# Two tiles of rows, each loaded in two halves of 64 rows through two queues

## The chip, the core and the metric

The kernel runs on one core of a Trainium2 chip. The core has a TensorE for matrix products (PE in the profile, with its weight loads as PEld), a VectorE (DVE), a ScalarE (ACT), a GpSimd (POOL) and a SyncE (SP); transfers between the chip's memory and the core's are started by instructions on the queues of SyncE, ScalarE or GpSimd, and are carried out by 16 DMA engines. The metric is the device time of one execution in microseconds, as the median of several runs.

## The reference

Two layers are computed on 2 x 512 rows of 512 numbers, in single precision, and only the final rows are returned. Cut to what matters:

```
x = L0_attn_hidden_states                       # (2, 512, 512)
x = layernorm(x + L0_attn(x))                   # linear attention with a fixed memory M, z
x = layernorm(x + L0_ffn(x))                    # gated, weights of three values, integers inside
x = layernorm(x + L1_attn(x))                   # softmax attention, one head of 128
x = layernorm(x + L1_ffn(x))                    # gated, 1376 wide

# L0_attn: of 32 query heads only every fourth is used (8 heads of 128)
q   = hidden @ Wq.T + bq ; sig_q = elu(q) + 1
num = sig_q @ M[h] ;  den = sig_q . z[h] + 1e-6
out = repeat(num / den, 4) @ Wo.T
```

What is changed lies ahead of the first product, the queries q of layer 0.

## The kernel before

The rows are held as eight tiles of 128 rows by 512 columns, `x_b_t` with batch b of 0 and 1 and tile t of 0 to 3 (256 KB each). TensorE needs them turned, so each 128 x 128 block is transposed by a matmul against an identity.

The queries of the first head and first batch are computed plainly, tile by tile, in `first_queries`: `first_rows(t)` transposes the four blocks of tile t (L454), then ScalarE copies one half of the result to `xt_raw` (L456) and VectorE the other (L457), and the same result is split into an upper and a lower part for the later heads (`xh_a` by ScalarE, L326; `xl_a` by VectorE, L327). Then four matmuls with the weights `wq[0]` (L473) add up the queries of that tile. All other heads are computed from split parts: `query_weights` splits a head's weights in three (ScalarE at L319, VectorE at L320 and L321, into `host_y` for head 1), and `passes` multiplies (L502), over the 512 rows of a batch at once. Behind them come the folding of M with Wo (L543), the reading of the memory (L557), the three other sublayers, and the stores of the eight output tiles (L1358, L1367).

At the very start TensorE has no data. It runs eight matmuls of ones (L113, the tile `rise`), each recorded as two passes, while the first rows are on their way.

Loads are issued in a written order. SyncE's queue issues, in this order: `x_0_0`, `wq0`, `x_0_2`, `x_0_3`, `wq1`, the small `bq` and `z`, `wq2`, the four tiles of batch 1, `wq3` to `wq7` (L385), `m`, and then the large weights. ScalarE's queue issues one load, `x_0_1`, as its first instruction, ahead of the loading of its function table. GpSimd issues none of these.

The framework gives each load issued by SyncE or ScalarE the next of eight completion counters in turn. An issue waits until the transfer that used its counter last has landed. So the first eight transfers go out without such a wait, and each later one stands behind the landing of the eighth transfer before it: `wq2`, the ninth, waits for `x_0_0`; `x_1_0` for `x_0_1`; `x_1_1` for `wq0`; `x_1_2` for `x_0_2`; `x_1_3` for `x_0_3`; `wq3` for `wq1`. The framework also puts the waits that order the work between the engines: the first transpose waits for `x_0_0` and the identity, the first transpose of the second tile for `x_0_1`, and so on.

The order of the other instructions on each engine is fixed when the kernel is built, partly by a scheduler with its own estimates and partly by hand (`issue_after`). Each engine works through its list in order.

Of the kernel before, what the change touches and what calls it, by code (L numbers as in the profile page):

```python
# [19 lines left out]
P = 128  # L20
# [19 lines left out]
def kernel(  # L40
# [19 lines left out]
    nc = tc.nc  # L60
# [27 lines left out]
    def load_x(b, tiles=range(NT)):  # L88
        for t in tiles:
            x = xp.tile([P, HID], F32, tag="x", name=f"x_{b}_{t}")  # L90
            eng = nc.scalar if b == 0 and t == 1 else nc.sync
            eng.dma_start(x, x_in[b, ts(t, P), :])
            xs[b].append(x)

    load_x(0, range(2))
    bq = const.tile([D, NH], F32, tag="bq", name="bq")
    z = const.tile([D, NH], F32, tag="z", name="z")
# [281 lines left out]
    with tc.tile_pool(name="a0w", bufs=1) as a0w, tc.tile_pool(name="a0", bufs=2) as a0:  # L379
        wq = []  # L380
        for h in range(NH):
            if h % 2 == 0:
                two = query_tile(f"wq{h}").rearrange("p a (k d) -> p a k d", k=NK)
            w = two[:, h % 2]
            nc.sync.dma_start(w, wq_in[h])  # L385
            wq.append(w)
            if h == 0:
                load_x(0, range(2, NT))
            elif h == 1:
                nc.sync.dma_start(bq, bq_in)  # L390
                nc.sync.dma_start(z, z_in)
            elif h == 2:
                load_x(1)
# [819 lines left out]
    t = NT - 1  # L1213
# [248 lines left out]
```

## Time and profile before

| | us |
|---|---|
| median of 3 runs (lowest, highest) | 459.4 (459.14, 459.92) |
| the profiled execution | 459.37 |
| its span, first to last instruction | 457.6 |
| TensorE busy in it | 449.9 (98%) |
| first matmul of ones; first transpose of rows | 1.05; 4.63 |
| `wq1` issued; landed | 2.59; 7.59 |
| ScalarE's first split of weights (L319) starts | 7.61 |
| first matmul from split parts (L502) starts | 11.33 |
| loads `x` on SyncE: issue to landing, median of 7 | 4.5 |
| load `x_0_1` on ScalarE: issue to landing | 3.3 |

The granted TensorE clock is 0.998 of full speed over the span. Times in the profile count from the start of the span. In a list of the chain or of the timeline the first number is the start, the second the length, both in us; in a list of waits the numbers are the total, how many times, and the longest; in a list of one line's instructions they are the shortest, median and longest duration in ns, and then the first and the last start in us. An instruction that issues a transfer stands under the queue's name (SPq, ACTq); the transfer itself is counted from the issue to its landing.

### The profile page before, as it was taken

To read this page: it belongs to the slowest core of one execution; us is meant where nothing else is said; L and a number is where in the kernel's file an instruction comes from. 1 tells how busy PE (TensorE), PEld (TensorE's weight loads), DVE (VectorE), ACT (ScalarE), POOL (GpSimd) and SP (SyncE) were. 2 spreads that over 40 slices of the span, in tenths; PEclk is the share of its full clock that TensorE was granted. 3 is DMA by queue.
4 is the path that set the end of the run, shared out by engine and by line. 5 is a ranking of instruction groups with operands and counts; after the bars stand their busy time and mean duration, and the time that the engine had idled before them with its cause. 6 is when DMAs were issued, how large, how long until landed. Compare 5 with 4: busy or idle time off the path is not lost.

```text
span 457.6 us, 5879 instructions
## 1 busy us (share of the span) xinstructions
PE 449.9 (98%) x1929; PEld 338.0 (74%) x1929; DVE 339.5 (74%) x665; ACT 270.2 (59%) x514; POOL 110.5 (24%) x149
## 2 busy tenths in 40 slices
PE   8999999999999999999999999999999999999995
PEld 8887754344588888888766578888888888888884
DVE  4966757667867888847978899795656778998632
ACT  4778995556567975567748544564755658442101
POOL 0300206565550069101362332000000000050101
PEclk9999999999999999999999999999999999999999
DMA  8999980000038101131585500000000000001001
GB/s 293 392 267 313 178 319 1 0 3 0 2 51 238 55 3 48 47 93 38 199 323 92 94 0 2 0 0 1 0 1 0 1 1 0 1 23 46 34 37 47
DMA packets 28693, 37.14 MB, mean 81 GB/s; under 512 B 16304, under 2 KB 17200, under 8 KB 28656
## 3 DMA queue, kind: packets, MB, share of 16 engines
q1 hardware_dynamic: 23216, 30.13, 19.2%
q0 software_dynamic: 1984, 5.77, 6.8%
q10 hardware_dynamic: 3456, 0.75, 0.8%
q8 instruction: 22, 0.36, 0.3%
q14 instruction: 15, 0.12, 0.1%
HBM read 32.45 MB, written 2.10 MB: 75 GB/s over the span
## 4 chain that ended last, share of the span: by engine, by line
PE 92%; DVE 3%; issue 2%; DMA 1%; ACT 1%; SPq 0%; POOL 0%; POOLq 0%; DVEq 0%
PE pm L1252 17%; PE po L557 10%; PE pq L502 9%; PE pg_f L735 9%; PE pu_f L735 9%; PE pc L1252 8%; PE pdm L1340 8%; PE pd_f L794 4%; PE pdc L1340 4%; PE pqk L1063 3%; PE pv L1080 2%; PE pot L1129 2%; PE po L1146 2%; PE psc L1019 2%; PE pmw L543 2%
## 5 line engine op out<-in xcount | busy, mean ns | idle before, releaser
L557 PE MATMUL po<-mw,q 128*128 128x512 f32 x128 | 57.1, 599 | 0.7 <-ACT den L561 0.4
L557 PEld LDWEIGHTS po<-mw,q 128*128 128x128 f32 x128 | 22.9, 189 | 33.4 <-issue 18.6
L146 POOL TENSOR_TENSOR rstd_f<-mv_f,ln_eps 128x1 f32<-128x1 f32 x15 | 4.4, 295 | 170.8 <-DVE mv_f L1355 130.2
L1252 PE MATMUL pm<-r,ugu 128*128 128x512 f32 x152 | 37.7, 389 | 0.0
L1252 PE MATMUL pm<-r,it_early 128*128 128x512 f32 x144 | 36.6, 392 | 0.0
L1252 PEld LDWEIGHTS pm<-r,ugu 128*128 128x128 f32 x152 | 28.5, 188 | 5.9
L170 ACT ACTIVATE ta_f<-y_f,below_half 128x512 int8<-128x512 f32 (+1 forms) x22 | 15.8, 720 | 27.2 <-DVE y_f L158 26.9
L1252 PEld LDWEIGHTS pm<-r,it_early 128*128 128x128 f32 x144 | 27.0, 188 | 6.0 <-issue 0.5
L579 DVE SCALAR_TENSOR_TENSOR x<-po,den,x 128x511 f32<-128x511 f32 x40 | 29.8, 745 | 2.1
L1262 DVE SCALAR_TENSOR_TENSOR ev_q<-pm,ev_q 128x512 f32<-128x512 f32 x27 | 18.5, 686 | 14.2 <-PE pm L1252 12.0
L574 POOL TENSOR_TENSOR y<-y,y 128x511 f32<-128x511 f32 x16 | 21.1, 1320 | 25.5 <-PE po L557 20.6
L761 DVE SCALAR_TENSOR_TENSOR it_f<-tb_f,ta_f 128x512 fp32r<-128x512 int16 (+1 forms) x22 | 15.2, 690 | 13.8 <-ACT tb_f L171 13.8
L735 PE MATMUL pg_f<-xh,tu 128*128 128x512 f32 x88 | 24.4, 399 | 0.0
L1261 ACT ACTIVATE ev_q<-pc 128x512 f32<-128x512 f32 x27 | 16.0, 594 | 14.1 <-PE pc L1252 14.0
L735 PE MATMUL pg_f<-xl,tu 128*128 128x512 f32 x88 | 23.6, 389 | 0.0
L735 PE MATMUL pu_f<-xh,tu 128*128 128x512 f32 x88 | 23.5, 389 | 0.0
L735 PE MATMUL pu_f<-xl,tu 128*128 128x512 f32 x88 | 23.5, 389 | 0.0
L1142 ACT ACTIVATE x<-x,off_f,rstd_f 128x512 f32<-128x512 f32 x7 | 5.7, 816 | 27.7 <-POOL off_f L1141 27.7
L561 ACT ACTIVATE den<-po,den_eps 128x1 f32<-128x1 f32 x64 | 13.9, 277 | 12.8 <-PE po L557 12.7
L349 POOL TENSOR_SCALAR td<-wd,inv_down 128x512 fp32r<-128x512 f32 x11 | 20.1, 1847 | 1.6 <-DVE inv_down L206 1.6
L794 PE MATMUL pd_f<-td,it_f 128*128 128x512 f32 x88 | 20.3, 389 | 0.0
L1252 PE MATMUL pc<-r,ugu 128*128 128x512 f32 x72 | 19.3, 390 | 0.0
(368 smaller groups left out, 1142.7 us busy)
## 6 DMA issues: line engine op xcount, KB each, us to landing
gu<-in_gu SPq DMA_DIRECT2D x20, 512.0 KB, 6.9
wd<-in_wd SPq DMA_DIRECT2D x20, 256.0 KB, 4.2
wo<-in_wo SPq DMA_DIRECT2D x8, 512.0 KB, 8.7
wo<-in_wo POOLq DMA_DIRECT2D x8, 512.0 KB, 9.8
wq<-in_wq SPq DMA_DIRECT2D x8, 256.0 KB, 4.6
x<-in_x SPq DMA_DIRECT2D x7, 256.0 KB, 4.5
out<-x SPq DMA_DIRECT2D x7, 256.0 KB, 2.0
x<-in_bo POOLq DMA_DIRECT2D x4, 256.0 KB, 5.9
```

The source lines that it names most:

```text
L170: nc.scalar.activation(a[:n], y, AF.Relu, bias=below_half[:n])
L349: eng.tensor_scalar(out, w, factor, None, ALU.mult)
L502: done = nc.tensor.matmul(p, w, x, start=(start and i == 0), stop=(i == len(todo) - 1), skip_group_check=not start,)
L557: nc.tensor.matmul(po, qs[b][h0 + j][:, ts(t, P)], mw[:, h0 + j, :], start=True, stop=True,)
L574: nc.gpsimd.tensor_add(ys[0][:, :LAST], ys[0][:, :LAST], y[:, :LAST])
L579: steps.append(nc.vector.scalar_tensor_tensor(x[:, :LAST], four[j][:, :LAST], d, x[:, :LAST], ALU.mult, ALU.add))
L735: nc.tensor.matmul(pp[a], t[:, a, i % NK, :], x2[b][i], start=(i == 0), stop=(i == 2 * NK - 1),)
L794: nc.tensor.matmul(pd, inter[b][c][:, ts(t, P)], td[c].bitcast(F32R), start=(c == 0), stop=(c == last),)
L1252: nc.tensor.matmul(p, w, x, start=(left[id(p)] == begun[id(p)]), stop=(left[id(p)] == 1))
L1261: nc.scalar.activation(ev, pc, AF.Copy, scale=CROSS)
L1262: nc.vector.scalar_tensor_tensor(ev, pm, MAIN, ev, ALU.mult, ALU.add)
L1340: nc.tensor.matmul(p[:, :w], got[j // 4][1][kind][:, j % 4], down_parts[j][kind][:, cols], start=(j == 0 and kind == kinds[0]), stop=(j == ...
```

## The change

In `load_x`, the tiles `x_0_0` and `x_0_1` are each loaded by two transfers of 64 rows (128 KB): rows 0 to 63 by SyncE's queue and rows 64 to 127 by ScalarE's. SyncE's list therefore starts with the first halves of both tiles and goes on with `wq0`; ScalarE's list starts with the two second halves. There are two transfers more in all, one on each queue. The other loads, the arithmetic and the number of the filler matmuls are as they were.

```diff
     def load_x(b, tiles=range(NT)):
         for t in tiles:
             x = xp.tile([P, HID], F32, tag="x", name=f"x_{b}_{t}")
-            eng = nc.scalar if b == 0 and t == 1 else nc.sync
-            eng.dma_start(x, x_in[b, ts(t, P), :])
+            if b == 0 and t < 2:
+
+                for eng, half in ((nc.sync, 0), (nc.scalar, 1)):
+                    at = t * P + half * P // 2
+                    eng.dma_start(x[ts(half, P // 2)], x_in[b, at : at + P // 2, :])
+            else:
+                nc.sync.dma_start(x, x_in[b, ts(t, P), :])
             xs[b].append(x)
 
     load_x(0, range(2))
```

Five lines are added, so line numbers of the changed kernel behind `load_x` are five higher.

## The prediction

> **What bounds the kernel now.** I read the first page of the profile, then the chain that ended last in order of time, then the waits, and last the first 14 us row by row, because every edit lies there. The page says which engine sets the end:
>
> ```profile
> span 457.6 us, 5879 instructions
> ...
> PE 449.9 (98%) x1929; PEld 338.0 (74%) x1929; DVE 339.5 (74%) x665; ACT 270.2 (59%) x514; POOL 110.5 (24%) x149
> ...
> PE 92%; DVE 3%; issue 2%; DMA 1%; ACT 1%; SPq 0%; POOL 0%; POOLq 0%; DVEq 0%
> ```
>
> TensorE is busy 98% of the span and is 92% of the chain. DMA is 1% of the chain, and the chain in order of time shows where that 1% lies:
>
> ```profile
> 2.12 0.43 SPq L92
> 2.55 0.04 issue
> 2.59 5.00 DMA wq<-in_wq
> 7.59 0.02 issue
> 7.61 0.63 ACT host_y L319
> ...
> 10.70 0.71 PE pq L473 x4
> 11.41 2.04 PE pq L502 x8
> ```
>
> The transfer on the chain is the weights of head 1 (call it wq1, the second load of line 385): issued by SyncE at 2.59 us and landed at 7.59. It isn't one of the two tiles that are edited. It is released to ScalarE's first step of the exact weights (L319). ScalarE works in order, so behind it stand the copies of row tiles 2 and 3 (L456), then VectorE's halves (L457), then TensorE's last four matmuls of the first head (L473, 10.70). From 11.41 on the chain is TensorE's own, without a transfer. So a microsecond by which wq1 lands later is a microsecond at the end, and the two tiles of rows count only if they reach this place. The waits of the first 14 us give the slack:
>
> ```profile
> DVE xt_raw L457 <- ACT xt_raw L456: 5.1, 2, 4.8
> ACT xt_raw L456 <- PE pt_a L454: 3.0, 1, 3.0
> ...
> ACT host_y L319 <- DMA wq<-in_wq: 0.2, 1, 0.2
> ```
>
> ScalarE stood idle for wq1 only 0.19 us (the timeline has the 0.2 as 0.19): that is all an earlier wq1 can give, since before it ScalarE is busy from 5.47 with copies that TensorE's first transposes released. What holds those transposes?
>
> ```profile
> L454 PEldq EVENT_SEMAPHORE  x1: 51/51/51, 3.9 to 3.9; - x1
> ...
> L473 PEldq EVENT_SEMAPHORE  x1: 51/51/51, 4.8 to 4.8; - x1
> ...
> 1.05 3.79 PE L113 MATMUL rise<-ones 128*128 128x128 f32 x16 [1.05 <-DVE below_half L108]
> 4.63 1.24 PE L454 MATMUL pt_a<-ident,x 128*128 128x128 f32 x8
> ```
>
> The first two lines are waits that TensorE's queue passes: at 3.9 for x_0_0, at 4.8 for the first weights. The next two are TensorE: the filler matmuls (L113) keep it busy until 4.84 by their modelled ends, and the transposes follow without a gap. x_0_0 had been there since 3.9 (issue 0.74 plus 3.2, the shortest latency of the x loads), x_0_1 since about 4.05 (0.74 plus 3.3). Both tiles are 0.5 us and more ahead of the engine that reads them.
>
> **The change part by part.** My sum is made against the profiled execution, 459.37 us: the span of 457.6 and 1.77 around it, which no edit touches. The median of the runs shown, 459.4, is 0.03 from it.
>
> *1. The tiles arrive in halves on two queues.* The bytes don't change: 256 KB each, with rows of 2 KB as before. The nearest row of the trace for such a split is the end of the kernel, where the last output tile leaves as 160 KB by SyncE and 96 KB by ScalarE, while the seven others leave whole:
>
> ```profile
> L1358 SPq DMA_DIRECT2D out<-x x7: 332/333/360, 407.8 to 448.1; - x7
> ...
> DMA to landing us min/median/max: 2.0/2.0/2.0
> ...
> DMA to landing us min/median/max: 1.8/1.9/2.0
> ```
>
> Whole tiles land in 2.0 us, the split one's parts in 1.8 and 2.0: the split gained between 0 and 0.2 us. The Trainium skill ("DMA: Bandwidth & Descriptors", "Rules for kernel authors") speaks against this change outright: two transfers to disjoint partition halves share the same DMA engines from one queue or from two, so one transfer of 128 partitions is to be used. By the row I'd book x_0_0 up to 0.2 us earlier (more is possible, since x_0_1's bytes no longer compete with it); by the rule nothing. The sum is the same by both: what is gained here lies under the filler matmuls, until 4.63 or so. If that cover were gone, it would be worth those 0.2 us. x_0_1 is now issued second on each queue, at 1.2 instead of 0.74, so at most 0.46 us later: 4.05 becomes 4.5 at the latest, and its transposes start at about 5.2. Cost 0, with 0.7 us to spare.
>
> *2. SyncE issues one load more ahead of wq0, x_0_2, x_0_3 and wq1.* One issue is 0.43 us plus a gap of 0.04, so these four go out 0.47 us later (wq1 at 3.06 instead of 2.59). ScalarE's second issue (0.41 by its own row) moves its table load from 1.19 to about 1.65, to end near 2.95; its next work comes at 5.47, so that is hidden. Does wq1 land 0.47 later? SyncE's issues before show what sets landings, since each later one stands behind one of these loads:
>
> ```profile
> SPq L92 <- DMA x<-in_x: 1.2, 2, 0.7
> ...
> SPq L385 <- DMA wq<-in_wq: 0.3, 1, 0.3
> ```
>
> By the rows of the timeline these waits end at 6.14 (x_0_2 landed), 6.94 (x_0_3) and 7.61 (wq1). The loads were issued 0.47 us apart and landed at 4.8, 6.1, 6.9 and 7.6, so 0.7 to 1.3 apart, and the time from issue to landing grew from 3.6 to 5.0. The DMA engines, not the issue, set the pace; their share in half-microsecond stretches is 1.02 to 1.21 from 2.5 to 4.5, with a dip to 0.70 at 4.5 to 5.0. The bytes ahead of wq1 are the same five tiles. So the later issue is hidden under the transfers in front of it. The bounds: all 0.47 is paid if the landing follows the issue; 0.19 is gained if wq1 comes so early that ScalarE doesn't wait. I take the value nearest to the pacing by engines, with a charge for two more transfers to be completed: the tiny loads bq and z landed 0.17 and 0.2 us after the one in front, which bounds what one more transfer with 128 rows of its own costs; the halves add no rows, so I charge a quarter of that each, 0.1 us together, an estimate. The others: wq0 is read at 5.89 (landed 4.8, at worst 5.25), x_0_2 at 6.79 (6.1, at worst 6.6), x_0_3 at 8.12 (6.9, at worst 7.4). All hidden.
>
> *3. Which issue waits for which landing.* The eight completion counters go round, so an issue waits for the eighth transfer before it. Two more transfers at the front mean that bq waits for the first half of x_0_0, z for the second, the third wq for one half of x_0_1 and x_1_0 for the other. bq had no wait and went out at 3.06; now it follows wq1 at 3.54 or when the half has landed, 3.9 at the latest by the row of before. Queued behind it on SyncE are z, wq2 and the four x_1 tiles, so wq2 goes from 4.01 to 4.5 or 4.8 and x_1_1 from 4.96 to 5.5 or 5.8. From x_1_2 on, each issue waits for the same transfer as before, the first until x_0_2's landing at 6.14, so the delay is swallowed there. wq2 is read at 11.18 (landed by about 8.6: 4.01 plus the median of 4.6), bq at 11.70 (7.76), x_1 from 13.06: over 1.3 us to spare in each. The fourth wq, at 12.84, is the closest: issued at 7.61, landed at about 12.2, and its issue hangs on wq1's landing in both kernels. Cost 0. After 11.41 the whole list of TensorE's waits has 0.4 and 0.3 us, for ScalarE and VectorE, and none for a transfer.
>
> *4. TensorE's extra waits.* Three more semaphore waits in front of the first transposes (two half tiles where there was one, twice). One takes 51 ns by the row above. They can run while the filler runs; if the one between the two tiles is paid, ScalarE's 0.19 idle before L319 takes it. Cost 0, at most 0.1.
>
> The order of all other instructions on each engine is the same in both builds. Sum: 0 + 0.1 + 0 + 0 = +0.1 us, so 459.5.
>
> **The rivals.** *wq1 follows its issue* (+0.47): for it, wq1 is the one load on the chain, with no slack, and the dip at 4.5 us says the DMA engines aren't full all the time; against it, the growing latency. It gives 459.8 to 459.9, which is within 0.2%. *wq1 gains*: if halves spread over two queues fill the slow start (78 GB/s at 1.5 to 2.0, 229 at 2.0 to 2.5), wq1 lands early and ScalarE's 0.19 is saved: 459.2. *Slower:* a load into 64 partitions moves at half the rate. The trace of before has no such load. 512 KB at the 380 GB/s of the full stretches take 1.38 us; at half rate 1.38 more, ahead of wq1 on the same engines, so wq1 lands near 9.0 and the end is 460.8 (+0.3%). It decides from 0.92 us on, that is, if the halves run below 0.6 of the rate. Against it: both halves are under way together and cover all partitions, and by the same page of the skill ("Why a DMA increments its semaphore by 16 and not by 1") 64 rows still go to all 16 engines; no run here shows it. *Faster by more than 0.2%:* no step of mine reaches 0.92 us; the named gains end at 0.19. What is left is that one profiled execution misleads me on the filler's cover or on later stages.
>
> **How the numbers follow.** 0.2% of 459.4, about what a measurement of this kernel can tell from no change, is 0.92 us. Chances: my sum 0.50, wq1 with its issue 0.10, the small gain 0.08 (all three within 0.2%: 0.68), half rate 0.20 (slower), something unseen that is faster 0.12. The time is that of the likeliest, 459.5. The range for 8 in 10: up to 460.8 for the half-rate case, down to 458.8, which is the 0.19 gained and the spread of the runs shown (459.14 to 459.92) below it.
>
> **What would show it.** In the profile after: TensorE's first transposes still at about 4.6, directly behind the filler; SyncE's issue of wq1 at 3.06 and ScalarE's L324 (L319 before) starting at 7.6 to 7.8; x_1_2's issue still near 6.1; the first L507 (L502) matmul near 11.4. If L324 starts near 8.1, landing follows issue; near 9, the halves are slow. Wrong altogether is the prediction if the start of the L507 matmuls moves by over 0.9 us, or if a stage behind 12 us changes length while its order is the same.

## The result, and the profile after

The changed kernel takes 460.5 us (median of 12 runs, 460.06 to 461.77); the kernel before took 459.52 beside it (12 runs, 459.08 to 459.92). The ratio is 1.0025, with a 95% interval of 1.0016 to 1.0034: 0.25% slower, some 1.1 us. The forecast was 459.5 and no change that can be measured. The time lies inside the stated range, but the kernel got slower, and by the prediction's own mark (the start of the L507 matmuls moving by over 0.9 us) its account of the first 12 us was wrong.

The first page of the profile after, the span and the engines' busy time:

```profile
span 459.1 us, 5882 instructions
...
PE 450.2 (98%) x1929; PEld 338.1 (74%) x1929; DVE 339.5 (74%) x665; ACT 270.2 (59%) x514; POOL 106.6 (23%) x149
```

All engines do the same work; the span is 1.5 us longer. Where it came from is seen by the starts of the stages in the two traces (us from the start of the span):

| | before | after | later by |
|---|---|---|---|
| first matmul from split parts (L502, now L507) | 11.33 | 12.45 | 1.12 |
| first matmul of the reading (L557, L562) | 62.8 | 63.9 | 1.1 |
| first matmul of the gated layer (L735, L740) | 121.7 | 122.8 | 1.1 |
| first matmul of the last layer (L1252, L1257) | 271.5 | 272.6 | 1.1 |
| last store issued (ScalarE, L1367, L1372) | 454.59 | 455.68 | 1.09 |
| end of the span | 457.6 | 459.1 | 1.5 |

Of the 1.5 us, 1.1 arise before 12.5 us and are carried on unchanged to the last store. The other 0.4 appear behind it, where nothing is computed. There SyncE ends the program with eight waits, as many as there are completion counters. What differs is how many of them are still to be passed when the last store has landed (2.0 us after its issue); the kernel before has two, the changed one all eight:

```profile
L1458 SPq EVENT_SEMAPHORE  x2: 28/28/28, 456.6 to 456.7; - x2
L1463 SPq EVENT_SEMAPHORE  x8: 27/28/28, 457.7 to 458.1; - x8
```

They start 0.06 us apart, so six more are 0.37 us. In the traces the stores take the counters in turn, like the loads, so each load that is added moves the last store's counter on by one. The number of waits left behind the last landing fits this: 2 in the five traces without an added transfer, 1 in the two with one more, 8 in the six with two more, 7 in the one with three (e5).

The other 1.1 us have to be explained from the start. The chain of the profile after, in order of time (start, length, what):

```profile
0.73 0.60 SPq L95
...
1.40 0.57 SPq L95
...
2.01 0.58 SPq L390
...
3.58 5.12 DMA wq<-in_wq
...
8.73 0.63 ACT host_y L324
...
11.82 0.71 PE pq L478 x4
12.53 2.03 PE pq L507 x8
```

It has the same shape as before, but SyncE's first three issues took 0.57 to 0.60 us where they had taken 0.38 to 0.43, and there is one more of them: wq1 went out at 3.58 instead of 2.59, and landed at 8.71 instead of 7.59. The instructions of the new line, with their durations in ns, show the halves' price on each queue:

```profile
L95 SPq DMA_DIRECT2D x<-in_x x2: 571/587/603, 0.7 to 1.4; - x2
L95 ACTq DMA_DIRECT2D x<-in_x x2: 626/736/847, 0.7 to 1.4; - x2
...
DMA to landing us min/median/max: 2.7/3.4/5.0
```

ScalarE's second took 0.85 us, and one half of the second tile needed 5.0 us, to 6.4. TensorE now waits for it, as its timeline (with the idle time before an instruction, and what ended it, in brackets) and ScalarE's show:

```profile
4.63 0.99 PE L459 MATMUL pt_a<-ident,x 128*128 128x128 f32 x4
6.46 0.66 PE L459 MATMUL pt_a<-ident,x 128*128 128x128 f32 x4 [0.85 <-DMA x<-in_x]
...
7.43 1.19 ACT L331 ACTIVATE xh_a<-pt_a 128x512 fp32r<-128x512 f32 x2
8.73 0.63 ACT L324 ACTIVATE host_y<-wq 128x512 fp32r<-128x512 f32 x1
```

ScalarE finishes with the second tile at 8.62 (it had been 7.42) and wq1 is there at 8.71. Two things are late by over a microsecond at the same place, and either would give nearly the whole 1.1 us. The experiments had to take them apart, and to find out why an issue of half the bytes takes longer.

### The profile page after: what moved, and what is told of

The parts are those of the page before. It is cut to its first block, busy times and chain, and to the rows that moved or that the text cites. A ratio compares the mean times of both kernels' runs of the same rounds, so it can differ in the third digit from the quotient of the medians.

```text
span 459.1 us, 5882 instructions
## 1 busy us (share of the span) xinstructions
PE 450.2 (98%) x1929; PEld 338.1 (74%) x1929; DVE 339.5 (74%) x665; ACT 270.2 (59%) x514; POOL 106.6 (23%) x149
## 4 chain that ended last, share of the span: by engine, by line
PE 91%; DVE 3%; issue 2%; DMA 1%; ACT 1%; SPq 1%; POOL 0%; POOLq 0%; DVEq 0%
PE pm L1257 17%; PE po L562 10%; PE pq L507 9%; PE pg_f L740 9%; PE pu_f L740 9%; PE pc L1257 8%; PE pdm L1345 8%; PE pd_f L799 4%; PE pdc L1345 4%; PE pqk L1068 3%; PE pv L1085 2%; PE pot L1134 2%; PE po L1151 1%; PE psc L1024 1%; PE pmw L548 1%
## 5 line engine op out<-in xcount | busy, mean ns | idle before, releaser
L562 PE MATMUL po<-mw,q 128*128 128x512 f32 x128 | 57.1, 599 | 0.7 <-ACT den L566 0.4
L562 PEld LDWEIGHTS po<-mw,q 128*128 128x128 f32 x128 | 22.9, 189 | 33.3 <-issue 18.6
L1257 PE MATMUL pm<-r,ugu 128*128 128x512 f32 x152 | 37.7, 389 | 0.0
L1257 PE MATMUL pm<-r,it_early 128*128 128x512 f32 x144 | 36.6, 392 | 0.0
L1257 PEld LDWEIGHTS pm<-r,ugu 128*128 128x128 f32 x152 | 28.5, 188 | 5.9
L1257 PEld LDWEIGHTS pm<-r,it_early 128*128 128x128 f32 x144 | 27.0, 188 | 6.0 <-issue 0.5
L740 PE MATMUL pg_f<-xh,tu 128*128 128x512 f32 x88 | 24.4, 399 | 0.0
L740 PE MATMUL pg_f<-xl,tu 128*128 128x512 f32 x88 | 23.6, 390 | 0.0
L740 PE MATMUL pu_f<-xh,tu 128*128 128x512 f32 x88 | 23.5, 389 | 0.0
L740 PE MATMUL pu_f<-xl,tu 128*128 128x512 f32 x88 | 23.5, 389 | 0.0
L1257 PE MATMUL pc<-r,ugu 128*128 128x512 f32 x72 | 19.3, 390 | 0.0
```

The source lines that it names most:

```text
L562: nc.tensor.matmul(po, qs[b][h0 + j][:, ts(t, P)], mw[:, h0 + j, :], start=True, stop=True,)
L740: nc.tensor.matmul(pp[a], t[:, a, i % NK, :], x2[b][i], start=(i == 0), stop=(i == 2 * NK - 1),)
L1257: nc.tensor.matmul(p, w, x, start=(left[id(p)] == begun[id(p)]), stop=(left[id(p)] == 1))
```

## Experiments

Theory A: two queues that issue at once hinder each other. Theory B: a transfer of 64 rows is itself dear to issue. Theory C: transfers to 64 neighbouring partitions move slowly, the prediction's slower rival. The ratios are to the kernel before on the same chip, whose median there was 460.2 to 460.3, so 0.1% is 0.46 us. In all of them the order of the instructions on each engine is that of the kernel before, apart from the loads, and nothing is left out of the computation.

**e1: all four halves on one queue**

```diff
-                for eng, half in ((nc.sync, 0), (nc.scalar, 1)):
+                for eng, half in ((nc.sync, 0), (nc.sync, 1)):
```

> The four halves all on SyncE's queue, none on ScalarE's. Theory A (two queues that issue at the same time slow each other's issues down: SyncE's took 0.60, 0.57 and 0.58 us and ScalarE's 0.63 and 0.85, where a lone one took 0.42): alone, each half is issued in 0.38 to 0.43 us, wq0 at about 2.6 and wq1 at about 4.0; the end is set by wq1 and lands between 460.3 and 461.2. Theory B (a transfer of 64 rows is itself dear to issue, some 0.6 us): wq1 is issued at about 4.7 and the end is above 461.2. Theory C (64 neighbouring partitions move at about half the rate, whichever queue): the share of the DMA engines is 0.8 to 0.9 but they move only about 200 GB/s while the halves are under way, as in the changed kernel.

Measured: 462.39 us, ratio 1.0040 (1.0027 to 1.0053). The chain:

```profile
0.73 0.60 SPq L95
...
1.40 0.57 SPq L95
...
2.01 0.60 SPq L95
...
3.29 0.59 SPq L390
...
4.87 4.52 DMA wq<-in_wq
```

Nothing is issued on ScalarE's queue, and each half still takes 0.57 to 0.60 us, and the whole load behind them 0.59. Theory A falls. The second tile lands early enough here that TensorE waits 0.24 us for it; ScalarE then stands 1.9 us for wq1 alone, and the time is 1.84 us longer (0.40% of 460.3), 0.38 of it behind the last store. Theory C's mark isn't met either: from 2.0 to 4.5 us the DMA engines are busy for 0.40 to 0.73 of the time, and divided by this share they move 307 to 370 GB/s, not about 200.

**e2: halves by columns**

```diff
-                    at = t * P + half * P // 2
-                    eng.dma_start(x[ts(half, P // 2)], x_in[b, at : at + P // 2, :])
+                    cols = ts(half, HID // 2)
+                    eng.dma_start(x[:, cols], x_in[b, ts(t, P), cols])
```

> The same two tiles on the same two queues, also in two transfers each, but cut by columns: all 128 rows, 256 columns each. Theory A: the number of simultaneous issues is the same, so issues stay near 0.6 us, wq1 is issued near 3.6 and the end is 460.2 to 460.8. Theory B: with 128 rows the issue takes 0.4, wq1 goes out at 3.06 and the end is at most 459.9. Theory C: all partitions are written by each transfer, so 3.0 to 4.5 us moves 350 to 400 GB/s instead of 200, the second tile lands by 4.6 and TensorE no longer waits 0.85 us for it; the end is below 460 unless wq1 itself is issued late.

Measured: 460.56 us, ratio 1.0014 (1.0004 to 1.0024). The issues take 0.38 to 0.45 us on both queues, wq1 goes out at 3.06 as B said, and the tiles land 2.7 to 3.1 us after their issues. The time was expected to be at most 459.9 against 459.5; it lost 0.6 us, 0.38 of it behind the last store. In the trace wq1 landed at 8.49, so the later issue by 0.47 us was not hidden, and more was lost on the way: in its trace the DMA engines moved 188 to 262 GB/s from 3.5 to 6.0, where before it was 238 to 397. B holds for the issue, and its number for the time was too low.

**e3: even and odd rows**

```diff
-                    at = t * P + half * P // 2
-                    eng.dma_start(x[ts(half, P // 2)], x_in[b, at : at + P // 2, :])
+                    rows = x_in[b, ts(t, P), :].rearrange("(p two) f -> p two f", two=2)
+                    eng.dma_start(x[half::2], rows[:, half, :])
```

> Two transfers of 64 rows per tile on the two queues as in the changed kernel, but one takes the even and the other the odd rows, so that each half spreads over all partitions. Theory A: as in the changed kernel, 460.2 to 460.8, issues near 0.6. Theory B (64 rows): the same as A, issues near 0.6. Theory C (neighbouring partitions): the rate at 3.0 to 4.5 us recovers to 350 to 400 GB/s, the second tile lands by 4.6, no wait of TensorE for it; the end is at most 460.0 if the rate was the cause, and unchanged if it was the issue.

Measured: 461.38 us, ratio 1.0025 (1.0013 to 1.0036), the same as the changed kernel. The issues are as dear as with neighbouring rows (0.57 to 0.62 on SyncE, 0.65 and 0.85 on ScalarE). The rate is not the same. First the half microseconds from 3.0 to 4.0 of the changed kernel, then those of e3, then those of e1 (start and end, length, the five engines' busy time, granted clock, share of the DMA engines, GB/s):

```profile
3.00:3.50 0.50, 0.50 (x4) 0.50 (x4) 0.00 (x0) 0.50 (x1) 0.00 (x0) 1.00 0.88 188
3.50:4.00 0.50, 0.50 (x5) 0.50 (x4) 0.00 (x0) 0.05 (x1) 0.00 (x0) 1.00 0.78 205
```

```profile
3.00:3.50 0.50, 0.50 (x4) 0.50 (x4) 0.00 (x0) 0.50 (x1) 0.00 (x0) 1.00 1.03 389
3.50:4.00 0.50, 0.50 (x5) 0.50 (x4) 0.00 (x0) 0.07 (x1) 0.00 (x0) 1.00 0.35 127
```

```profile
3.00:3.50 0.50, 0.50 (x4) 0.50 (x4) 0.00 (x0) 0.00 (x0) 0.00 (x0) 1.00 0.46 152
3.50:4.00 0.50, 0.50 (x5) 0.50 (x4) 0.00 (x0) 0.00 (x0) 0.00 (x0) 1.00 0.67 242
```

Divided by the share, the changed kernel's engines moved 214 and 263 GB/s while busy, e3's 378 and 363. But e1's, with nothing but halves of neighbouring rows under way, moved 330 and 361, and the changed kernel's own moved 380 from 2.5 to 3.0, with the halves of the first tile. So there is a slow stretch, at 0.57 to 0.72 of e3's rate, but it is not shown that neighbouring rows cause it. By the ratio its absence brought no time back. In e3's own trace the second tile landed at 5.5 and L507 started only 0.45 us later than in the kernel before; the rest of its loss lies elsewhere (the table behind e12).

**e4: only the first tile in halves**

```diff
-            if b == 0 and t < 2:
+            if b == 0 and t < 1:
...
-                nc.sync.dma_start(x, x_in[b, ts(t, P), :])
+                eng = nc.scalar if b == 0 and t == 1 else nc.sync
+                eng.dma_start(x, x_in[b, ts(t, P), :])
```

> Only the first tile in halves; the second is whole on ScalarE's queue, behind its half. SyncE issues no load more ahead of wq1 than before the change. Theory A: while ScalarE issues its two loads SyncE's first three issues take 0.6, so wq1 goes out at about 3.0 instead of 2.59, and the end is 459.6 to 460.1. Theory B: only one half on SyncE is dear, wq1 at about 2.8; 459.6 to 459.9. Theory C: half of the slow bytes are gone, so half the loss stays: about 460.0.

Measured: 461.43 us, ratio 1.0028 (1.0019 to 1.0038). All three theories expected too little. wq1 goes out at 2.95, only 0.36 us late. But the second tile, whole, stands on ScalarE's queue behind a half: its issue takes 0.83 us, it lands about 6.0, and TensorE's wait for it is the longest of the runs:

```profile
4.36 0.60 PE L460 MATMUL pt_a<-ident,x 128*128 128x128 f32 x4
6.03 0.66 PE L460 MATMUL pt_a<-ident,x 128*128 128x128 f32 x4 [1.07 <-DMA x<-in_x]
```

ScalarE is held by the second tile here, and not by wq1. But the matmuls from split parts (L508) start at 11.79, only 0.46 us later than in the kernel before. The trace is one of the shorter executions (460.65), and most of the loss of 1.3 us is not located at the start by it.

**e5: the issue by itself, 145 us into the program**

```diff
             wd = wdp.tile([P, HID], F32, tag=f"wd{c}", name=f"wd{name}_{c}")
-            nc.sync.dma_start(wd[:n], wd_in[i : i + n, :])
+            src = wd_in[i : i + n, :]
+            if name == "0" and c == 4:
+                nc.sync.dma_start(wd[:64], src[:64])
+                nc.sync.dma_start(wd[64:], src[64:])
+            elif name == "0" and c == 6:
+                nc.sync.dma_start(wd[:, :256], src[:, :256])
+                nc.sync.dma_start(wd[:, 256:], src[:, 256:])
+            elif name == "0" and c == 8:
+                nc.sync.dma_start(wd[0::2], src[0::2])
+                nc.sync.dma_start(wd[1::2], src[1::2])
+            else:
+                nc.sync.dma_start(wd[:n], src)
```

> The kernel before, with three loads of the first feed-forward's down weights cut in two, all on SyncE's queue, some 140 us after the start: chunk 4 into two transfers of 64 neighbouring rows, chunk 6 into two of 256 columns, chunk 8 into even and odd rows; whole chunks between them. It measures the issue by itself. If a transfer of 64 rows is dear to issue whatever stands around it, those of chunks 4 and 8 take about 0.6 us each (and the whole one behind them perhaps too) and those of chunk 6 about 0.4, like the whole ones. If the price belongs to the first microseconds of the program, all take 0.33 to 0.43. No effect on the end is expected by either: 459 to 461.

Measured, SyncE's timeline (L258 and L259 are the halves of 64 rows, L261 and L262 the halves by columns, L264 and L265 the even and odd rows, L267 whole loads):

```profile
144.44 0.56 SPq L258 DMA_DIRECT2D wd<-in_wd  x1
145.03 0.60 SPq L259 DMA_DIRECT2D wd<-in_wd  x1
145.67 0.58 SPq L267 DMA_DIRECT2D wd<-in_wd  x1
146.30 0.43 SPq L261 DMA_DIRECT2D wd<-in_wd  x1
146.78 0.43 SPq L262 DMA_DIRECT2D wd<-in_wd  x1
147.26 0.42 SPq L267 DMA_DIRECT2D wd<-in_wd  x1
147.72 0.50 SPq L264 DMA_DIRECT2D wd<-in_wd  x1
148.64 0.48 SPq L265 DMA_DIRECT2D wd<-in_wd  x1
```

A load of 64 rows takes 0.56 to 0.60 us to issue, the whole load behind it 0.58, a whole load or a half by columns 0.42 or 0.43. The even and odd rows take 0.48 to 0.50, less than expected; but SyncE had waited in front of the second, and a whole load issued after a wait takes 0.33 (as at 6.14 in the kernel before), so they too are dearer. Theory B is shown away from the start of the program, with one queue. The single time, 463.38 us, is not used.

**e6: the later issue alone, with whole tiles**

```diff
-            eng = nc.scalar if b == 0 and t == 1 else nc.sync
-            eng.dma_start(x, x_in[b, ts(t, P), :])
+            nc.sync.dma_start(x, x_in[b, ts(t, P), :])
```

> Both tiles whole and both on SyncE's queue, so that wq0, x_0_2, x_0_3 and wq1 stand behind one issue more (wq1 at 3.06 instead of 2.59) and no transfer is cut. It is my step 2 alone. If the DMA engines set the landing, wq1 lands at 7.5 to 7.8 and the matmuls of L502 start at 11.2 to 11.5, as before. If the landing follows the issue, wq1 lands at about 8.05 and they start at about 11.8.

Measured: 460.72 us, ratio 1.0012 (1.0003 to 1.0022), 0.55 us longer. Nothing is cut, and wq1 goes out 0.47 us later. The profiled execution (460.32, among the shorter of 22) lost nothing at the start: wq1 landed at 7.4 and the first matmul from split parts started at 11.12. What it lost, it lost at about 66 us (the table behind e12). By the times the later issue may count; by this one trace it doesn't. A single execution can't settle a step of half a microsecond here.

**e7 and e8: wq1 issued ahead of x_0_3, in the kernel before and in the changed one**

```diff
             if h == 0:
-                load_x(0, range(2, NT))
+                load_x(0, range(2, NT - 1))
             elif h == 1:
+                load_x(0, range(NT - 1, NT))
                 nc.sync.dma_start(bq, bq_in)
```

> The kernel before with wq1 issued ahead of x_0_3 (2.12 and 2.59 us). wq1 should land at about 6.9 and x_0_3 at 7.6, half a microsecond ahead of its transposes. ScalarE's 0.19 us in front of L319 goes: L502 starts at about 11.15 and the end is 0.2 us earlier, which the times hardly show. If x_0_3 comes late instead, TensorE waits for it near 8.1 and nothing is gained or up to 0.3 lost.

> The changed kernel with wq1 issued ahead of x_0_3. If wq1 alone sets the end of the front, 0.4 to 0.6 us come back (L324 at about 8.2, L507 at about 11.9). If the second tile, which landed at 6.4, holds ScalarE as long as wq1 does, its copies and upper parts end at 8.6 whatever wq1 does, and at most 0.15 us come back: L507 at 12.3 or later.

Measured: e7 459.94 us, ratio 0.9994 (0.9984 to 1.0004), no verdict; its trace even has wq1 landing at 7.95 and TensorE waiting 0.33 us for x_0_3. e8 461.02 us, ratio 1.0028 (1.0017 to 1.0038). In e8, wq1's issue came back from 3.58 to 3.11 and no time came with it. Its profiled execution (460.37; the shortest of 22 is 460.35) has ScalarE starting L324 at 7.58, directly behind the second tile's upper parts and without a wait for wq1, while TensorE waits 0.46 us for the second tile. L508 starts at 11.28, no later than in the kernel before, so here a second tile that lands at 5.5 costs nothing at the start. What the median lost is not located by this trace, beyond 0.38 us behind the last store.

**e9: wq1 on ScalarE's queue, in the kernel before**

```diff
             w = two[:, h % 2]
-            nc.sync.dma_start(w, wq_in[h])
+            (nc.scalar if h == 1 else nc.sync).dma_start(w, wq_in[h])
```

> The kernel before, with wq1 issued by ScalarE's queue as its second load, at about 1.2 us instead of 2.59; SyncE's later loads each move 0.47 us ahead. If the end follows wq1's issue wherever ScalarE waits for it, the time falls by the idle time in front of L319, 0.2 us by the profile of before and perhaps 0.3 to 0.4 in other executions; it can't fall by the 1.4 us of the issue, since the second tile's copies keep ScalarE busy until 7.4. If x_0_2 (read at 6.79) is pushed behind wq1 and lands late, the gain is lost: 0 to 0.4 us slower.

Measured: 459.76 us, ratio 0.9990 (0.9982 to 0.9998), 0.5 us shorter than the kernel before. The build put wq1 first on ScalarE's queue (0.74) and x_0_1 second (1.18), the other way round than I had written. ScalarE's waits in the first 14 us have no transfer any more:

```profile
ACT xt_raw L456 <- PE pt_a L454: 2.8, 2, 2.6
ACT L456 <- PEq L1447: 1.7, 1, 1.7
ACT xh_a L326 <- DVE xt_raw L457: 1.3, 2, 0.8
```

By the median the gain is a little more than the 0.2 us by which one trace had ScalarE waiting, in the trace it is 0.15 (L502 at 11.18). It is the version that beats both kernels, by an interval that only just excludes no change.

**e10 and e11: both kernels once more, unchanged**

> The changed kernel once more, for a second profiled execution and for its ratio beside the other runs of this call. Issues of the halves again 0.57 to 0.85 us and wq1 at 3.58; ratio 1.002 to 1.003. The landing of the second tile (6.4 before) may lie between 5.4 and 6.4, as e3 and e8 had it; the start of the L507 matmuls between 11.4 and 12.5.

> The kernel before once more, for a second profiled execution: issues as in the first, 0.38 to 0.43 us, wq1 at 2.59; landing of wq1 7.2 to 8.0 and the start of the L502 matmuls 11.1 to 11.7, which shows how far single executions differ in the front.

Measured: the changed kernel 461.13 us, ratio 1.0027 (1.0016 to 1.0037), the loss of the first comparison again. In the second trace of the kernel before, wq1 landed by 7.22 and ScalarE didn't wait for it; L502 starts at 11.19. The second trace of the changed kernel starts L507 at 13.3, later than I had expected. The second tile landed at 6.3 as in the first, but more went with it (durations in ns, shortest, median, longest):

```profile
L459 PEld LDWEIGHTS pt_a<-ident,x x16: 141/230/230, 4.4 to 11.1; 128*128 128x128 f32 x16
L459 PE MATMUL pt_a<-ident,x x16: 273/421/472, 4.6 to 11.2; 128*128 128x128 f32 x16
```

In the first trace the median was 273 ns and only the first three took 421. Here most take 421, until about 9.8, and then the duration falls to 273.

**e12: only the second tile in halves**

```diff
-            if b == 0 and t < 2:
+            if b == 0 and t == 1:
```

> Only the second tile in halves; the first is whole on SyncE's queue, and ScalarE issues only one half. SyncE: x_0_0 at 0.74, the half at 1.18 (0.6), wq0 at 1.8 (0.6), wq1 at about 3.4, 0.8 later than before. ScalarE's half goes out first, so the second tile should land by about 5. If wq1's issue alone can cost the time, the loss is about 0.8 us (ratio 1.0017). If the late second tile was needed for the loss, it is 0.3 or less.

Measured: 460.86 us, ratio 1.0016 (1.0007 to 1.0025), as expected for wq1's issue alone. ScalarE issues a single half, both halves land 3.2 to 3.5 us after their issues, and TensorE runs its first eight transposes without a wait for a tile. The chain:

```profile
1.81 0.58 SPq L390
...
3.57 4.96 DMA wq<-in_wq
...
8.55 0.63 ACT host_y L324
```

wq1 goes out at 3.57 here because x_0_3's issue took 0.62 in this execution. ScalarE waits 0.54 us for wq1. With the second tile in time, the late wq1 alone costs 0.7 us; in the trace L507 starts 0.94 us later than before.

**Where each trace put its time.** In all traces but e5's, which changes a later stage too, three places make up the difference to the first trace of the kernel before, to within 0.3 us: the first matmul from split parts, the stage of the reading (from the first matmul of L557 to that of L735), and the time from the last store's issue to the end. In us:

| trace | split parts start later by | the reading is longer by | behind the last store, more by | span, more by |
|---|---|---|---|---|
| before, second (e11) | -0.14 | 0.76 | 0.00 | 0.70 |
| changed | 1.12 | -0.02 | 0.37 | 1.46 |
| changed, second (e10) | 1.96 | 0.95 | 0.38 | 3.37 |
| e1, four halves on one queue | 1.79 | 1.39 | 0.38 | 3.61 |
| e2, columns | 0.91 | 0.00 | 0.38 | 1.35 |
| e3, even and odd rows | 0.45 | 1.50 | 0.38 | 2.40 |
| e4, first tile only | 0.46 | 0.90 | -0.06 | 1.29 |
| e6, whole tiles, one queue | -0.21 | 1.06 | 0.01 | 0.96 |
| e7, swap in the kernel before | 0.37 | 0.43 | 0.00 | 1.05 |
| e8, swap in the changed kernel | -0.05 | 0.45 | 0.38 | 0.98 |
| e9, wq1 on the other queue | -0.15 | 0.00 | 0.00 | -0.14 |
| e12, second tile only | 0.94 | 0.00 | -0.06 | 0.99 |

The second place was in neither the prediction nor the experiments. ScalarE waits there, at about 65 us, for a load of the first feed-forward's weights; in e11:

```profile
ACT tu L347 <- DMA gu<-in_gu: 0.7, 1, 0.7
```

Where the table has 0.00 or -0.02 there is no such wait, elsewhere it is 0.3 to 1.4 us and the reading is longer by about as much. Each of the two kernels has one trace without it and one with 0.7 or 0.8, so they don't tie it to the change. How often it falls in the executions that were not profiled is not known, so the medians of the variants may carry it in different measure.

## Why the prediction was wrong, by its own steps

What failed first of all is step 2: it had wq1 go out 0.47 us later and land 0.1 later, with the rest hidden. It went out 0.99 later, landed 1.12 later, and L507 started 1.12 later. Step 3 was booked with nothing and cost 0.37. That the time, 460.5, still lies inside the range is luck: its upper end, 460.8, was put there for the half rate, and the case that wq1 follows its issue was priced at 459.8 to 459.9.

**Step 1, the tiles.** Right that an early first tile is worth nothing: the transposes of x_0_0 still start at 4.63, behind the filler. Wrong that x_0_1 lands at 4.5 at the latest. It landed at 6.4, and at 5.5 to 6.4 in all five traces where ScalarE issues a half and then a second load (the changed kernel twice, e3, e4, e8). The bound allowed for one issue of 0.46 us and took the time to landing over from a lone first load (3.3). The measured issue of the first is 0.63, of the second 0.83 to 0.85, and the landing follows 4.1 to 5.0 later. Where ScalarE's second load is not behind a half of 64 rows (e2, e9), it is in time. Why this one is so slow to land is open: in the five traces the load of ScalarE's function table also moves to 2.27, among the transfers, where it lay at 0.73 to 1.67 in the others, and no run takes the two apart.

**Step 2, SyncE's issues.** The sum took 0.43 us for each issue from whole loads, with one issue more, so 0.47. The measured shift is 0.99: 0.47 for the one issue more, and 0.52 because three are dearer (the first 0.60 instead of 0.38, the second 0.57 instead of 0.43, wq0 behind them 0.58 instead of 0.42). I had costed a half by the duration of a whole, although no load of 64 rows stood in the trace; this unknown should have had bounds of its own. And even the 0.47 were not hidden. The growing time from issue to landing (3.6 to 5.0 us) looked like a queue of transfers that swallows a later issue. The times say otherwise: by ratio, 0.47 later costs 0.55 us (e6, whole tiles), 0.98 later 0.7 (e12), 2.28 later 1.5 (e1, without the 0.38 behind the last store). The traces of e12 and e1 agree, with L507 later by 0.94 and 1.79; that of e6 does not (0.21 earlier). In single traces wq1 lands 4.3 to 5.8 us after its issue, which hides a step of 0.47. The rival that wq1 follows its issue was nearly right in its slope, as far as these medians show it, and its size was wrong for the same mis-sized term.

**Step 3, the counters,** did no harm at the start, though the delay was larger than said: wq2 waited for the late second tile and went out at 6.44, not at 4.5 or 4.8, and the stage up to L562 still kept its 51.5 us. But the step looked at the loads alone. The same turn of the counters reaches the last store, and the six waits more behind it cost 0.37 us. **Step 4, TensorE's extra waits,** cost what was said or less.

**The rival at half rate** had its price (460.8) near the result, for a reason that the runs don't bear out: e1 has the halves without the low rate and loses more, and e3 has the rate restored and is as slow by the ratio. The weighed rule of the Trainium skill ("DMA: Bandwidth & Descriptors", "Rules for kernel authors": don't split by partition halves, use one transfer) was right in its advice. The prediction read it as "no gain"; the runs show a loss, through a price of issue and a turn of the counters that the rule doesn't mention.

**How the parts add up.** By the ratio the changed kernel lost some 1.15 us. Behind the last store lie 0.37 of it, in both of its traces. The late wq1 alone costs 0.7 (e12, where it goes out at 3.57 as in the changed kernel, and where the last store is followed by no waits more). Together this is 1.1, so the late second tile adds nothing that the medians show: it ends at ScalarE's L324 like wq1, and only the later of the two counts. The sum fits, but with intervals of about 0.4 us each way it is no proof. It also leaves e4 and e8 open. Both lost 1.3 us by the ratio, though wq1 went out only 0.36 and 0.52 us late; the second tile, late in both, and the wait at 65 us are candidates, and their single traces, both among the shorter executions, don't decide.

## What to carry to other kernels

Count an issue by its shape as well as by its number: here a load of 64 rows took 0.14 to 0.22 us more to issue on SyncE than one of 128, though it moved half the bytes, and made the next one dear too, while a cut by columns did not. Look ahead of the critical load on its own queue before adding anything there: moving that load to the other queue's front gained 0.5 us, while splitting loads that nobody waited for lost 1.1. When two late things meet at one in-order engine, an experiment that mends one of them can show nothing; do each alone. And read every variant's trace stage by stage to its very end before its median is put down to one cause: here a third of the loss lay behind the last store, and a wait at 65 us came and went in the traces of the same kernel.

## What the runs showed of the hardware that was not expected

- The issue of a transfer of 64 rows by 2 KB: 0.56 to 0.60 us on SyncE and 0.60 to 0.65 on ScalarE, the next transfer on the same queue 0.56 to 0.59 and 0.83 to 0.85, against 0.38 to 0.45 for 128 rows of 2 KB or of 1 KB. What in the issue takes this time is open.
- From 3.0 to 4.0 us the DMA engines of the changed kernel moved 214 to 263 GB/s per full share, with even and odd rows 363 to 378, with four halves of neighbouring rows on one queue 330 to 361. The cause of the slow stretch is open.
- Two transfers more at the start of the program put 0.37 us behind its last store, through the turn of the completion counters.
- A hole in the start seems to cost more than itself. In e10 TensorE stood still from 5.69 to 6.38 and then worked at 421 ns per transpose until about 9.8, instead of 273. The Trainium skill ("TensorE: Matmul & The Clock Gate", "Part 1: The HAM clock gate") has the array's clock rise only after some 3.4 us of sustained work, counted in windows that don't start with the kernel; 3.4 us after 6.38 is 9.8, which agrees. The granted clock of those stretches reads 1.00 in the profile, so only the durations show it there. In the other trace of the changed kernel the hole was longer (0.85 us), but the durations had begun to fall in front of it, and the transposes behind it already took 273 ns. It is one trace.
